# Three attentions of a four-layer transformer kernel: groups that alternate, instead of layer after layer

## The chip, the cores and the metric

The kernel runs on one core of a Trainium2 chip. The metric is device time in microseconds (us), the median of several runs. A core has five engines that each work through their own list of instructions in order: PE (TensorE, matmuls, with a weight load PEld beside it), DVE (VectorE), ACT (ScalarE), POOL (GpSimd) and SP (SyncE, which here only issues DMAs). A line number such as L561 is a line of the kernel before the change.

## The reference, cut to what matters

`x` has 32 sequences of 128 tokens and 128 features. Four layers follow one another, each an attention and a feed-forward, added through a tanh gate. The change touches layers 0 and 1 alone:

```
x = x + tanh(g) * L0_xattn(ctx, layernorm(x), bias, seq_len)   # 16 heads of 8, keys and values from ctx, masked by length
x = x + tanh(g) * L0_ffn(layernorm(x))                        # 128 -> 512 -> 512 -> 512 -> 128, SiLU gate, two GELUs
x = x + tanh(g) * L1_xattn(layernorm(x), ctx, w_qkv, w_proj)  # 16 heads of 8, keys = ctx and own, so 256 keys
x = x + tanh(g) * L1_ffn(layernorm(x))                        # begins with a causal attention, 16 heads of 4, then 2 of 8 experts
...                                                           # layer 2 (attention, experts) and layer 3
```

A sequence depends on no other, up to the experts. So the work on one group of sequences can go ahead of another's, as long as each group passes the steps in order.

## The kernel before, in words

**Groups and jobs.** The 32 sequences are eight groups of four (`NB`). A job is one attention for one group. The loop `attend` (L916) takes a list of jobs. Before, it is 24 jobs, layer by layer: layer 0's attention for groups 0 to 7, then layer 1's for 0 to 7, then the causal one inside layer 1's feed-forward (called 1f) for 0 to 7.

**A job** (`attention`, L536) has four units of four heads and two steps a unit, so eight steps. A step first computes scores (PE `sc` L561; a causal row L584 first in 1f) for the maxima (DVE L592 or L597). The maxima are split in three bfloat16 parts, transposed (`tpn` L611) and written by a DMA into rows 96 to 98 of the query tile (L615), so that a second product of the same parts, with keys and queries exchanged (`sct` L561), gives scores less their maximum. ACT takes the exponential (L627); in 1f POOL then sets the later positions to zero (L630); PE multiplies with the values (`av` L644), whose extra column of ones gives the sum, and the result is divided (L650 to L659). Layer 1's steps have two score tiles instead of one.

**Operand tiles.** Queries and keys are kept in DRAM as three bfloat16 parts and loaded as stacks (`Stacks.load`, L386) into ring buffers (`Slots`, L346): four query tiles `stack_q` and four each of `stack_k` and `stack_l`. Rows 0 to 71 (0 to 35 in 1f) hold the parts. In layer 0, rows 72 to 74 of the key hold the bias and masks; the query rows 64 to 95 hold ones. As the three layers share the tiles, the first jobs of layer 1 and of 1f have POOL set rows to zero (`ready` and `take`, L360 to L370).

**The pipe** (`Pipe`, L446) sets the order. `turn` (L486) runs once a step: weights four steps after the scores, products one step after that, one step of `before` (the preparation of the next job: normalization, projections, splitting in parts), one of `after` (what follows a finished job), and `beside` (L479), which takes pieces of the `fill`. The fill is layer 0's feed-forward (`mlp0`, L1012): it is appended when a group's first attention is done. It yields after every eight rows or so of matmul: SiLU pairs, then eight GELU pieces (PE L1037, ACT L1040), then the last product (L1046). At one piece a step it lags behind the attention and ends in layer 1's stage. A layer 1 job for a group can't begin before that group's feed-forward is done (L1068), and a 1f job not before layer 1's job of that group (L1114).

A scheduler then places the emitted instructions in the engines' lists, so that a piece can move some steps from where it was emitted.

**Shared rooms.** `shared` (L936) gives everything but scores and products two psum banks under one tag, `h`: transpositions, projections, the feed-forward. Tag `scr` has two buffers, `y` three.

**Clears.** Each feed-forward piece also issues one DMA of zeros (`cleared`, L995) into the table from which the experts later read, until 40 are out. SP issues these, in order with all loads.

**What follows.** After the 24 jobs come layer 1's experts, layer 2's attention with its own pipe, layer 2's experts, and layer 3.

Of the kernel before, what the change touches and what calls it, by code (L numbers as in the profile page):

```python
# [12 lines left out]
F32 = mybir.dt.float32  # L13
F32R = mybir.dt.float32r
BF = mybir.dt.bfloat16
# [7 lines left out]
P = 128  # L23
NB = 4
# [2 lines left out]
EPS = 1e-5  # L27

LOTS = dict(r1=(0, 8, 512), r2=(0, 8, 512))
MAGIC = 12582912.0  # L30


# [40 lines left out]
def tile_flamingo_gated(  # L73
# [20 lines left out]
    nc = tc.nc  # L94
    B = x.shape[0]
    NG = B // NB
# [16 lines left out]
    xs = []  # L113
# [23 lines left out]
    ones = CST(cst, "ones")  # L137
# [52 lines left out]
    with tc.tile_pool(name="prep", bufs=1) as pp, tc.tile_pool(name="prep_ps", bufs=2, space=PSUM) as ppp:  # L190
        for name, bias in (("bias0", bias0), ("bias2", bias2)):
            parts = pp.tile([P, 3, B], BF, tag=f"parts_{name}", name=f"parts_{name}")
            rest = pp.tile([P, B], F32, tag="rest", name=f"rest_{name}")
            split3(parts[:, 0], parts[:, 1], parts[:, 2], bias, rest)
            tp = ppp.tile([3 * B, P], BF, tag="tp", name=f"tp_{name}")
            nc.tensor.transpose(tp, parts.rearrange("p a b -> p (a b)"), ident_b)
            rows = pp.tile([3 * B, P], BF, tag=f"rows_{name}", name=f"rows_{name}")
            nc.vector.tensor_copy(rows, tp)
            kept = dram.tile([3, B * P], BF, name=f"kept_{name}")
            nc.sync.dma_start(out=kept.rearrange("a (b k) -> (a b) k", k=P), in_=rows)  # L200
            bias_rows[name] = kept


    def rsqrt(pool, v, eps=EPS):
# [141 lines left out]
    class Slots:  # L346


        def __init__(self, pool, name, n, blocks=4, ones=(96, 99), engines=(nc.vector, nc.gpsimd)):
            self.at, self.tiles, self.readied = 0, [], {}  # L350
            for i in range(n):
                t = pool.tile([P, blocks, NB, P], BF, name=f"stack_{name}{i}", bufs=1)
                eng = engines[i % len(engines)]
                rows = t.rearrange("p m b k -> p (m b k)")
                eng.memset(rows, 0.0)
                if ones:
                    eng.memset(rows[ones[0] : ones[1]], 1.0)
                self.tiles.append(t)

        def ready(self, rows, value):  # L360

            for i in range(len(self.tiles)):
                self.readied.setdefault(i, []).append((rows, value))

        def take(self):
            i = self.at % len(self.tiles)
            self.at += 1
            for rows, value in self.readied.pop(i, []):
                nc.gpsimd.memset(self.tiles[i].rearrange("p m b k -> p (m b k)")[rows], value)
            return self.tiles[i]  # L370

    class Stacks:

# [2 lines left out]

        def __init__(self, H, d, queries, keys, bias=None, readied=()):

            self.bias, self.slots, self.readied = bias, [queries] + keys, readied
            self.H, self.halves = H, max(1, d // 8)
            self.d = d // self.halves
            self.ahead = {}

        def load(self, n, parts, at, group):  # L386

            t = self.slots[n].take()
            heads = slice(0, 9 * self.d)
            for e in range(self.halves):  # L390
                dst = t[heads, 4 * e : 4 * (e + 1)]
                if n == 0:
                    first = (self.H * e + 4 * at) * NB * P
                    src = parts.rearrange("d c h n -> (d c) (h n)")[:, first : first + 4 * NB * P]
                    nc.sync.dma_start(
                        out=dst.rearrange("p m b k -> p (m b k)"),
                        in_=src[:, None, :].to_broadcast([3 * self.d, 3, 4 * NB * P]),
                    )
                else:
                    src = parts.rearrange("(h e) d a (c n) -> e (d a c) h n", e=self.halves, n=NB * P)[e]  # L400
                    nc.sync.dma_start(
                        out=dst.rearrange("p m b k -> p m (b k)"), in_=src[:, 4 * at : 4 * (at + 1)]
                    )
            if n and self.bias:
                rows = bias_rows[self.bias][:, group * NB * P : (group + 1) * NB * P]
                nc.sync.dma_start(
                    out=t[72:75, 0:4].rearrange("p m b k -> p m (b k)"),
                    in_=rows[:, None, :].to_broadcast([3, 4, NB * P]),
                )
            return t  # L410

        def loads(self, group, q, keys, at):
            for slots, rows, value in self.readied:
                slots.ready(rows, value)
            self.readied = ()
            return self.load(0, q, at, group), [self.load(i + 1, k, at, group) for i, k in enumerate(keys)]


# [117 lines left out]
    def attention(banks, r, g, q, keys, values, o, following=None, causal=False):  # L536
# [18 lines left out]
        def product(dst, stat, mov, b, start, whole):  # L555

            n = r.halves
            for h in range(4):
                for e in range(n):
                    rows = slice(0, P if whole and e == n - 1 else 96)  # L560
                    nc.tensor.matmul(  # L561
                        dst[:, h * P : (h + 1) * P], lhsT=stat[rows, 4 * e + h, b], rhs=mov[rows, 4 * e + h, b],
                        start=start and h == e == 0, stop=h == 3 and e == n - 1, skip_group_check=True,
                    )

        def unit(u):
# [41 lines left out]
            def placed(negp, dq):  # L608

                tp = psum.tile([48, P], BF, tag="tp", name="tpn")  # L610
                nc.tensor.transpose(tp, negp.rearrange("p c x -> p (c x)"), ident_b)  # L611
                rows = pool.tile([48, P], BF, tag="mrows", name="mrows")
                nc.vector.tensor_copy(rows, tp)
                first = 4 * (r.halves - 1)
                nc.sync.dma_start(  # L615
                    out=dq[96:99, first : first + 4].rearrange("p h b q -> p (h b) q"), in_=rows
                )

            def weights(bp):
# [283 lines left out]
    class Layer:  # L903

        def __init__(self, stacks, before, given, after, causal=False, ahead=1):

            self.ahead = ahead
            self.stacks, self.before, self.given, self.after, self.causal = stacks, before, given, after, causal  # L910

        def begin(self, g):
# [3 lines left out]
    def attend(pipe, banks, jobs):  # L916
# [8 lines left out]
        for i, (layer, g) in enumerate(jobs):  # L925
            if i in ends:
# [2 lines left out]
            parts = attention(  # L929
                banks, layer.stacks, g, *layer.given(g), (lambda: then.begin(n)) if then else None, layer.causal  # L930
            )
            due = jobs[i + 1 : i + 1 + layer.ahead] if i == 0 else jobs[i + layer.ahead : i + 1 + layer.ahead]
            pipe.run(parts, chain(*[a.before(m) for a, m in due]), lambda layer=layer, g=g: layer.after(g))
        pipe.drain()
# [39 lines left out]
    with ExitStack() as stack:  # L974
# [11 lines left out]
        def layer0():  # L986
# [2 lines left out]
            h1 = W0(w0, "h1").rearrange("p (c o) -> p c o", c=4)  # L989
            h2 = W0(w0, "h2").rearrange("p (c o) -> p c o", c=4)  # L990
            w3 = W0(w0, "w3").rearrange("p (c o) -> p c o", c=4)
            zeros = mlp.tile([P, 512], F32, name="zeros")
            nc.gpsimd.memset(zeros, 0.0)

            def cleared():  # L995
                if clear:
                    t = clear.pop(0).rearrange("n p m -> p n m")
                    nc.sync.dma_start(out=t, in_=zeros[:, None, 0 : t.shape[2]].to_broadcast(list(t.shape)))

            def before(g):  # L1000
                y = layernorm(pool, xs[g], bufs=3)
                kT = pool.tile([P, NB * P], F32, tag="xT", name="kT", bufs=1)
                nc.sync.dma_start(out=kT, in_=ctx_kT[:, g * NB : (g + 1) * NB, :])
                yield
# [5 lines left out]
                at[g] = q, [k], [va], o  # L1010

            def mlp0(g):  # L1012
                y = layernorm(pool, xs[g], bufs=3)
                yield
                xT = mlp.tile([P, NB * P], F32, tag="xT", name="xT")
                nc.vector.tensor_copy(xT, flat(transposed(psum, y)))
# [38 lines left out]
                return  # L1055
                yield

            return Layer(stacks, before, lambda g: at[g], after)

        done = set()  # L1060

        def layer1():
            stacks = Stacks(16, 8, queries, [keys0, keys1], readied=[(queries, slice(64, 96), 0.0)])
            qkv = WA(wa, "qkv")
            at = {}

            def before(g):
                while g not in done:  # L1068
                    pipe.advance(pipe.fill)
                y = layernorm(pool, xs[g], bufs=3)  # L1070
                yield
                xT = pool.tile([P, NB, P], F32, tag="xT", name="xT", bufs=1)
                nc.scalar.copy(xT, transposed(psum, y))
# [29 lines left out]
                add_gated(xs[g], 1, po)  # L1103
                done.add(8 + g)

            return Layer(stacks, before, lambda g: at[g], after)

        def layer1f():
            cleared = [(keys1, slice(i, i + 32), 0.0) for i in (32, 64)]
            stacks = Stacks(16, 4, queries, [keys1], readied=cleared)  # L1110
            at = {}

            def before(g):
                while 8 + g not in done:  # L1114
                    pipe.advance(pipe.afters)
                y, h = layernorm(pool, xs[g], bufs=3, again="scr")
                yield
                hT = pool.tile([P, NB, P], F32, tag="scr", name="hT")
                nc.scalar.mul(hT, transposed(psum, h), COL(col, "g1"))
# [51 lines left out]
                    nc.tensor.matmul(pl[:, b, :], lhsT=tT[:, b, :], rhs=WA(wa, "router"), start=True, stop=True)  # L1171
                yield from routes1.take(pool, psum, g, pl, t, 5, 0.0)

            return Layer(stacks, before, lambda g: at[g][:4], after, causal=True)

        layers = layer0(), layer1(), layer1f()
        attend(pipe, banks, [(layer, g) for layer in layers for g in range(NG)])


    tail = ctx.enter_context(tc.tile_pool(name="tail", bufs=1))  # L1180
# [448 lines left out]
```

## Time and profile before

| what | us |
|---|---|
| median of 3 runs (2176.64 to 2182.37) | 2178.75 |
| the profiled execution, time | 2170.34 |
| its span | 2168.5 |
| PE busy in the span (76%) | 1658.0 |
| DVE busy (55%) | 1197.4 |
| ACT busy (41%) | 894.0 |
| POOL busy (29%) | 638.6 |
| ACT table loads ahead of exponentials, 72 of them | 92.4 |
| 16 DMA engines, share of their time for SP's queue | 34.0% |

A page gives busy time per engine, then the span in 40 slices with a digit for the busy tenths and for the granted clock of PE. The trace answers for a stretch of time, and lists groups of instructions as "line engine operation out<-in, count | busy us, mean ns | idle before, and what ended it". A wait is listed as who waited for whom, with its total us, how often, and the longest. In a busy PE row the ends of matmuls are modelled, so that rows overlap; the distance of two starts tells the pace.

### The profile page before, as it was taken

The numbers are of one execution on the slowest core, as the hardware profiler recorded it, in microseconds if no ns is written. First come the engines' busy times: TensorE is split into PE (matmuls) and PEld (weight loads), VectorE is DVE, ScalarE is ACT, GpSimd is POOL, SyncE is SP. The second block draws the span as 40 slices with busy tenths as digits, with TensorE's granted clock in tenths as the row PEclk, the third lists the DMA queues.
The fourth block names the chain that finished last, engine by engine and source line by source line (L and its number), as shares of the span: only waits on it lengthen the run. The fifth ranks groups of instructions, "written<-read, shape, count | busy, mean of one in ns | idle before, by whom it ended". The sixth has DMA issues, their size and how long they took to land.

```text
span 2168.5 us, 35498 instructions
## 1 busy us (share of the span) xinstructions
PE 1658.0 (76%) x13624; PEld 1010.3 (47%) x13624; DVE 1197.4 (55%) x3504; ACT 894.0 (41%) x1110; POOL 638.6 (29%) x637
## 2 busy tenths in 40 slices
PE   0599998989999999878777569926666629995355
PEld 0455445456656666555455424414555514442223
DVE  7645446475545476766666433357667631113797
ACT  0376565565787745333323223301111204441244
POOL 5101101020000012454544482056443430003550
PEclk9999999999999999987877779966667759997566
DMA  6564558634332343112212035435344212332110
GB/s 214 154 230 154 187 184 266 219 101 124 105 100 67 94 145 84 51 54 59 56 48 55 25 116 174 141 104 148 110 124 121 71 63 101 135 132 86 41 49 20
DMA packets 164536, 244.66 MB, mean 113 GB/s; under 512 B 20560, under 2 KB 102288, under 8 KB 164112
## 3 DMA queue, kind: packets, MB, share of 16 engines
q1 hardware_dynamic: 156176, 225.62, 34.0%
q0 software_dynamic: 8192, 16.79, 2.7%
q8 instruction: 107, 1.75, 0.4%
q14 instruction: 61, 0.50, 0.1%
HBM read 139.74 MB, written 101.24 MB: 111 GB/s over the span
## 4 chain that ended last, share of the span: by engine, by line
PE 40%; DVE 14%; POOL 13%; issue 8%; ACT 2%; DMA 2%; SPq 0%; POOLq 0%; DVEq 0%; ACTq 0%
PE ye L851 5%; PE ph L1382 4%; PE av L644 4%; POOL by_expert_r L699 4%; PE sct L561 4%; POOL got L886 3%; PE sc L561 3%; PE ph L1037 3%; PE p L1203 2%; PE tpe L838 2%; DVE mx L592 2%; PE p L1205 2%; PE tp L282 1%; POOL r L208 1%; POOL w L249 1%
## 5 line engine op out<-in xcount | busy, mean ns | idle before, releaser
L627 ACT ACTIVATE w<-sct 128x1024 f32<-128x1024 f32 x288 | 292.8, 1024 | 346.4 <-PE sct L561 345.2
L592 DVE TENSOR_REDUCE mx<-sc 128x8 f32<-128x1024 f32 x160 | 194.9, 1220 | 130.0 <-PE sc L561 129.6
L561 PEld LDWEIGHTS <-stack_q 96*128 96x128 bf16 x2560 | 194.4, 110 | 134.5 <-issue 104.3
L886 POOL DMA_INDIRECT got<-by_expert_r,slot_r x128 | 127.7, 998 | 360.8 <-issue 335.0
L597 DVE TENSOR_REDUCE mx<-sc 128x4 f32<-128x1024 f32 x128 | 152.9, 1222 | 132.8 <-PE sc L561 132.3
L644 PE MATMUL av<-w,va 128*9 128x128 f32 (+2 forms) x3584 | 198.1, 295 | 36.7 <-POOL w L630 31.9
L561 PE MATMUL sc<-stack_k,stack_q 96*128 96x128 bf16 x1536 | 145.7, 244 | 46.8 <-DMA stack_k<-k 17.4
L561 PE MATMUL sct<-stack_q,stack_k 128*128 128x128 bf16 (+1 forms) x1536 | 139.5, 236 | 17.3 <-DVE mx L592 8.3
L561 PEld LDWEIGHTS <-stack_k 128*128 128x128 bf16 (+1 forms) x1536 | 111.8, 107 | 69.6 <-issue 66.6
L644 PEld LDWEIGHTS av<-w,va 128*9 128x9 f32 (+2 forms) x3584 | 98.6, 94 | 87.5 <-POOL w L630 43.5
L851 PE MATMUL ye<-hid,w 128*128 128x512 f32 x276 | 133.4, 593 | 2.3 <-DVE hid L1208 2.3
L311 POOL CAST hml<-whole 128x512 bf16<-128x512 f32 (+1 forms) x48 | 30.1, 626 | 343.0 <-ACT whole L310 166.7
L1037 PE MATMUL ph<-h,w 128*128 128x512 f32 x256 | 123.7, 610 | 1.8 <-ACT hn L1040 0.9
L1037 PE MATMUL ph<-hn,w 128*128 128x512 f32 x256 | 121.2, 604 | 0.7 <-ACT hn L1040 0.7
L208 POOL TENSOR_TENSOR r<-r,m 128x4 f32<-128x4 f32 x56 | 58.5, 1044 | 188.8 <-DVE r L207 175.0
L561 PE MATMUL sc<-stack_l,stack_q 96*128 96x128 bf16 x1024 | 110.4, 238 | 0.0
L650 ACT COPY ot<-av 128x512 f32<-128x512 f32 x112 | 65.5, 584 | 99.5 <-PE av L644 96.6
L630 POOL TENSOR_SCALAR_AFFINE_SELECT w<-w 128x1024 f32<-128x1024 f32 x64 | 70.8, 1106 | 113.9 <-ACT w L627 113.7
L561 PE MATMUL sct<-stack_q,stack_l 128*128 128x128 bf16 x1024 | 98.9, 234 | 2.7 <-DVE mx L592 2.7
L627 ACT ACT_TABLE_LOAD x72 | 92.4, 1283 | 9.7 <-PE sct L561 8.5
L699 POOL DMA_INDIRECT by_expert_r<-yn,slot_r x64 | 65.6, 1025 | 83.1 <-DVE slot_r L757 25.4
L656 PE MATMUL tpo<-cst,ot 128*128 128x128 f32 x448 | 82.4, 306 | 9.5 <-ACT ot L650 6.9
(295 smaller groups left out, 3290.5 us busy)
## 6 DMA issues: line engine op xcount, KB each, us to landing
by_expert_r<-zeros SPq DMA_DIRECT2D x40, 1024.0 KB
stack_q<-q SPq DMA_DIRECT2D x96, 288.0 KB
stack_k<-k SPq DMA_DIRECT2D x96, 288.0 KB
k<-hml SPq DMA_DIRECT2D x16, 1152.0 KB
w<-in_e_dram SPq DMA_DIRECT2D x23, 514.5 KB
xt<-by_expert_r SPq DMA_DIRECT2D x46, 256.0 KB
by_expert_r<-yt SPq DMA_DIRECT2D x46, 256.0 KB
q<-hml SPq DMA_DIRECT2D x72, 128.0 KB
```

Source lines behind the costliest of these rows:

```text
L208: nc.gpsimd.tensor_tensor(r, r, m05.to_broadcast([P, NB]), ALU.pow)
L561: nc.tensor.matmul(dst[:, h * P : (h + 1) * P], lhsT=stat[rows, 4 * e + h, b], rhs=mov[rows, 4 * e + h, b], start=start and h == e == 0, s ...
L592: latest["maxima"] = nc.vector.tensor_reduce(mx[:, :, b0 : b0 + 2].rearrange("p h b -> p b h"), sc.rearrange("p i (h k) -> p i h k", h=4), ...
L597: nc.vector.tensor_reduce(mx[:, :, b0], sc.rearrange("p i (h k) -> p h i k", h=4), AX.XY, ALU.max, negate=True,)
L627: latest["weights"] = nc.scalar.activation(w.rearrange("p i h k -> p i (h k)"), sc, AF.Exp)
L644: nc.tensor.matmul(av[32 * h : 32 * h + dv + 1, b * P : (b + 1) * P], lhsT=values[c][:, b, 4 * u + h, :], rhs=w[:, i, h, :], start=c == 0, ...
L656: nc.tensor.transpose(tp[:, b].rearrange("p s r -> p (s r)"), ot[:, b, :], ident)
L699: ins = nc.gpsimd.indirect_dma_start(out=self.rows(), out_offset=bass.IndirectOffsetOnAxis(ap=slots, axis=0), in_=rows, in_offset=None,)
L851: nc.tensor.matmul(y, lhsT=w2[:, f, :], rhs=hid[:, f, :], start=f == 0, stop=f == n_f - 1)
L886: ins = nc.gpsimd.indirect_dma_start(out=got[:, k, b, :], out_offset=None, in_=self.rows(), in_offset=bass.IndirectOffsetOnAxis(ap=self.sl ...
L1037: nc.tensor.matmul(ph, lhsT=wt[:, c, f * P : (f + 1) * P], rhs=h[:, c, :], start=c == 0, stop=c == 3)
L1382: nc.tensor.matmul(ph, lhsT=E2(w, "w1")[:, f * P : (f + 1) * P], rhs=xT, start=True, stop=True)
```

## The change

1. **Order.** The 24 jobs are no longer layer by layer but in the list `ORDER`: five of layer 0, then jobs of layer 1, layer 0 and 1f in turn; it ends with three of 1f.
2. **Rates.** `beside` takes 0.875 pieces a step in jobs of layer 0 and of 1f and 0.5 in jobs of layer 1, instead of 1.
3. **Shared tiles.** As the layers now use the tiles in turn, POOL zeroes no rows between the stages any more: every load of layer 1's first key tile also brings three rows of zeros, and every load of 1f's key brings three rows of ones at rows 36 to 38, where 1f's maxima now go. Its products take 36 and 39 rows instead of 96 and 128. POOL's twelve memsets are gone; two small DRAM rows of zeros and ones are made at the start.
4. **Clears.** The tile of zeros has 256 columns instead of 512, and each clear is two DMAs of half the size.
5. **Buffers.** `y` has four buffers instead of three.

```
+ORDER = [
+    (0, 0), (0, 1), (0, 2), (0, 3), (0, 4), (1, 0), (0, 5), (1, 1), (2, 0), (1, 2), (0, 6), (1, 3),
+    (2, 1), (1, 4), (0, 7), (2, 2), (1, 5), (2, 3), (1, 6), (2, 4), (1, 7), (2, 5), (2, 6), (2, 7),
+]
+RATES = 0.875, 0.5, 0.875
...
+        for name, value in (("zeros", 0.0), ("ones", 1.0)):
+            rows = pp.tile([3, NB * P], BF, tag=f"rows_{name}", name=f"rows_{name}")
+            nc.vector.memset(rows, value)
+            bias_rows[name] = dram.tile([3, NB * P], BF, name=f"kept_{name}")
+            nc.sync.dma_start(out=bias_rows[name], in_=rows)
...
-            for rows, value in self.readied.pop(i, []):
-                nc.gpsimd.memset(self.tiles[i].rearrange("p m b k -> p (m b k)")[rows], value)
...
+            self.parts = 9 * self.d
+            self.top, self.end, self.all = (36, 36, 39) if self.d == 4 else (96, 96, P)
...
-            if n and self.bias:
-                rows = bias_rows[self.bias][:, group * NB * P : (group + 1) * NB * P]
+            if n and self.beside[n - 1]:
+                rows = bias_rows[self.beside[n - 1]]
+                if rows.shape[1] > NB * P:
+                    rows = rows[:, group * NB * P : (group + 1) * NB * P]
                 nc.sync.dma_start(
-                    out=t[72:75, 0:4].rearrange("p m b k -> p m (b k)"),
+                    out=t[self.parts : self.parts + 3, 0:4].rearrange("p m b k -> p m (b k)"),
...
-                    rows = slice(0, P if whole and e == n - 1 else 96)
+                    rows = slice(0, r.all if whole and e == n - 1 else r.end)
...
+            pipe.fills[0] = (pipe.fill, layer.rate)
...
-            zeros = mlp.tile([P, 512], F32, name="zeros")
+            zeros = mlp.tile([P, 256], F32, name="zeros")
...
-                    t = clear.pop(0).rearrange("n p m -> p n m")
-                    nc.sync.dma_start(out=t, in_=zeros[:, None, 0 : t.shape[2]].to_broadcast(list(t.shape)))
+                    t = clear.pop(0).rearrange("n p (i m) -> i p n m", m=256)
+                    for half in (t[0], t[1]):
+                        nc.sync.dma_start(out=half, in_=zeros[:, None, :].to_broadcast(list(half.shape)))
...
-                y = layernorm(pool, xs[g], bufs=3)
+                y = layernorm(pool, xs[g], bufs=4)
...
-            return Layer(stacks, before, lambda g: at[g], after)
+            return Layer(stacks, before, lambda g: at[g], after, rate=RATES[0])
...
-            stacks = Stacks(16, 8, queries, [keys0, keys1], readied=[(queries, slice(64, 96), 0.0)])
+            stacks = Stacks(16, 8, queries, [keys0, keys1], "zeros", None)
...
-            cleared = [(keys1, slice(i, i + 32), 0.0) for i in (32, 64)]
-            stacks = Stacks(16, 4, queries, [keys1], readied=cleared)
+            stacks = Stacks(16, 4, queries, [keys1], "ones")
...
-        attend(pipe, banks, [(layer, g) for layer in layers for g in range(NG)])
+        attend(pipe, banks, [(layers[i], g) for i, g in ORDER])
```

## The prediction

> **What bounds it now.** I read the page's 40 slices first, then busy time by stage, then the stretches job by job, then PE's waits. Jobs are one attention for one group; I cut the stages at the first exponential (ACT w L627) of each layer: layer 0's attention 71.3 to 480.4, layer 1's to 881.8, layer 1's second ("1f", causal) to 1225.7, everything later 942.8 us.
>
> ```profile
> PE   0599998989999999878777569926666629995355
> PEclk9999999999999999987877779966667759997566
> ```
>
> Slices 2 to 16 are full of PE at the whole clock; slices 17 to 23 (1f) are not. Busy time by stage (columns: stretch, its us, busy us of PE, PEld, DVE, ACT, POOL, granted clock, DMA share, GB/s):
>
> ```profile
> 71.30:480.40 409.10, 369.14 (x2827) 202.83 (x2826) 219.14 (x585) 248.32 (x270) 49.78 (x68) 0.97 0.57 187
> 480.40:881.80 401.40, 385.37 (x4690) 253.70 (x4687) 240.01 (x510) 266.76 (x295) 52.07 (x68) 1.00 0.37 101
> 881.80:1225.70 343.90, 270.21 (x2599) 176.26 (x2595) 221.70 (x718) 110.37 (x150) 168.23 (x168) 0.81 0.19 51
> 1225.70:2168.50 942.80, 622.33 (x3452) 369.67 (x3452) 467.52 (x1590) 263.98 (x391) 335.34 (x298) 0.76 0.33 100
> ```
>
> No other engine is over 70% in any of the first three. PE is the bound in layers 0 and 1; in 1f PE is short of ready work and runs at 0.81. Why, from PE's waits in 1f (total, times, longest):
>
> ```profile
> PE av L644 <- POOL w L630: 30.5, 27, 3.4
> PE sc L584 <- DVE mx L592: 12.7, 14, 3.8
> PE tp L282 <- DVE t L1165: 9.7, 7, 2.7
> ```
>
> These are chains (exponential, POOL's causal mask, product) with nothing independent between. The feed-forward of layer 0 is independent, but it is used up by 757 us.
>
> **PE work at full clock.** Recorded durations overlap, so I count by the distance of starts, in layer 1's timeline:
>
> ```profile
> 607.67 3.65 PE L1037 MATMUL ph<-h,w 128*128 128x512 f32 x8
> 611.15 0.33 PE L561 MATMUL sc<-stack_k,stack_q 96*128 96x128 bf16 x3
> ...
> 616.87 0.39 PE L561 MATMUL sc<-stack_k,stack_q 96*128 96x128 bf16 x4
> 617.09 0.39 PE L561 MATMUL sc<-stack_l,stack_q 96*128 96x128 bf16 x4
> ```
>
> 3.48 us for eight fp32 rows of 512: 0.43 each (3.44 a piece of eight). 0.22 for four score rows: 0.056 each. Likewise av 0.037, fp32 rows of 128 0.11, tpn 0.17, the causal row of 512 0.22. One feed-forward group has 88 rows of 512 and 8 transposes: 37.8+0.9 = 38.7 us, in 11 pieces. A job of layer 0: 128 score rows 7.2, 128 av 4.7, 20 transposes 2.2, tpn 0.7 = 14.8. Layer 1: 256 scores 14.3, 256 av 9.5, transposes 2.6, projections 3.5, tpn 0.7 = 30.6. 1f: 7.2+4.7, 16 masks 3.5, transposes 3.1, projections 4.3+2.6, tpn 0.7 = 26.1. Layer 1's stage holds 184 of the 512 rows of L1037, so 2.9 of eight feed-forwards; layer 0's 5.1. Filling of PE by stage: (118+197)/409 = 77%; (245+112)/401 = 89%; 209/344 = 61%.
>
> What a job costs without any feed-forward: layer 0 33.5 (the first one), layer 1 (39.4+42.2+39.1)/3 = 40.2, 1f a mean of 45.7 over seven, and 23.9 for the last. The covered stretch 104.8 to 757.2 (layer 0's jobs 1 to 7, layer 1's 0 to 4, all feed-forwards) holds 104+153+310 = 567 us of work in 652.4 us: 87%.
>
> **The change, part by part.** *The order and the rates.* Nothing of the attention or feed-forward work is added or removed; pieces move. In the order in which the changed program issues ACT's instructions I counted SiLU pairs and GELUs between the exponentials: of 80 such pieces 45 stand in layer 0's jobs, 18 in layer 1's, 17 in four 1f jobs ((2,0) to (2,3): 4, 6, 4, 3). The last piece is in (2,3). So 18 jobs are covered; six are not: (1,6), (2,4), (1,7), (2,5), (2,6), (2,7). Before, eight 1f jobs and about three of layer 1 were bare. Sum: job (0,0) 33.5; the other 17 covered jobs hold 7x14.8+6x30.6+4x26.1+310 = 702 us. At 85% filling that is 826. Bare: 2x40.2+3x45.7+23.9 = 241. Together 1100.5 against 1154.4: -54. I take 85%, under the 87% shown, because a covered 1f job brings its POOL chain; at 93% (layer 1's stretch 519.8 to 757.2: 122+112 in 237, near 99%, shows that high is possible) it is 755: -125; at 78% (layer 0's stage) 900: +20.
>
> *The covered 1f job closely:* 26.1+17/4x3.44 = 41 us of work against 45.7 bare, if the clock comes back to that of covered jobs (0.97 to 1.00). If it stayed 0.81, the four jobs' 162 us of work would be 200: +38. I take the former, since layer 1's stage ran at 1.00.
>
> *ACT.* The two programs have 150 table loads each, so the sum does not change, but GELUs now stand among 1f's exponentials, which POOL's masks and then PE wait for:
>
> ```profile
> L1040 ACT ACT_TABLE_LOAD x30 | 38.5, 1283 | 0.5
> L1040 ACT ACTIVATE hn<-ph,col 128x512 f32<-128x512 f32 x41 | 28.2, 687 | 45.4 <-PE ph L1037 45.2
> ```
>
> A piece costs ACT up to 0.69+2x1.28 = 3.3 us, 14 in a 1f job that has 14.5: 28 of 48. The Trainium skill, page "ScalarE: Activation LUTs", section "Table sets: the hidden batching unit", speaks against the change: activations should be batched by table set, and it gives about 2.7 us a load. By its figure a piece is 6.1, the job 14.5+26 = 40 of 48, and ACT would nearly bind (my 85% would fall to about 80%). The trace's 1.28 decides.
>
> *POOL.* 1f's 64 scatters (L699, 1.07 us each, 8.5 a job) stand among its masks; a 1f job's scatters fall due in the job after it, which for (2,0) to (2,4) is one of layer 0 or 1 without masks. A gain of up to 8 us over these jobs that I leave inside the 85%.
>
> *Clears.* 40 transfers of 1 MB become 80 of 0.5 MB with packets of 1 KB instead of 2 KB. The trace's packets in this stretch took 91 ns (2 KB) and 60 ns (1 KB): 20,480x91/16 = 116 us of the 16 engines' time becomes 154, +38 over some 400 us whose share is 0.57. Hidden behind PE while the share stays under 1; where it is a burst, stack_k and stack_q loads queue behind it. Bounds 0 and +15; I take +2. SP: 40 more issues at 0.50 and 64 row loads (zeros or ones for the keys) at 0.33: 41 us on a queue that spends 341 of 1154 issuing. A row load follows the key load of a tile that is wanted two units later; behind it on SP stand the maxima (stack_q<-mrows) and the next unit's loads, which PE's sct wants four steps later, so I take 0 (up to +6: 64 landings, each 0.1 late). Three clears now stand ahead of the first q and k writes behind the weights' load: 0 to +5, I take +2.
>
> *Stacks.* Twelve POOL memsets of 1.8 us go (4 at 433 to 475, 8 at 848 to 881); they held SP's stack_q loads up to 18 us, but PE's rows show no wait on them: 0 (down to -6). Score rows in 1f contract 36 or 39 partitions instead of 96 or 128; rows of 96 and 128 both took 0.22 us, so 0. y gets a fourth buffer, which keeps 1f's held residual from blocking: 0. Two DVE memsets at the start, under 0.5 each: +1.
>
> Sum: -54+5 = -49. Against the profiled execution (span 2168.5, time 2170.3) that is 2121; the median of the runs is 8.4 above the profiled one, so 2130.
>
> **Rivals.**
> *A, main case (0.58):* filling 82 to 89%, 2093 to 2163.
> *B, more (0.12):* mixed jobs fill as layer 1's stretch did, 93% and over: 2059 to 2093. For it: 97 to 99% has been reached. Against: layer 0's jobs with as many pieces had 84%.
> *C, the pieces pay in 1f what they paid before (0.14).* In layer 0 57 pieces cost 409-8x33.5 = 141: 2.5 each, 72% of their PE time although a bare job left PE idle for half. If they cost 2.5 in 1f and the clock gives nothing back, the sum is only the +5 of side costs: 2184; with half of the clock back (6 us a job, four jobs, halved: -12) 2172. Of its 0.14, 0.06 lies under 2172, 0.07 within 0.3%, 0.01 above.
> *D, slower (0.16): psum.* Two banks, tag h, serve every transposition, projection and feed-forward product of all three layers. A covered 1f job takes them some 12 times for itself and 5 or 6 for pieces, where a bare one took 12, and a bank is held until ACT or DVE, in order behind exponentials, has read it. PE is in order: a wait for a bank holds the scores behind it. At 0.7 us more for each of 4x18 uses the -50 is gone; at 1.0, 72-49 = +23: 2202. Against: layer 1's covered jobs took them some 15 times in 59 us with almost no PE wait.
> *That the order isn't followed:* excluded by the issue order above: the jobs alternate and the pieces are spread.
>
> **Numbers.** A measurement tells 0.3%, 6.5 us. Faster: A, B and 0.06 of C = 0.76. Within: 0.07 of C and 0.02 of D = 0.09. Slower: 0.01 of C and 0.14 of D = 0.15. The range leaves out half of B (0.06) and most of D above 2190 (0.12): 2080 to 2190.
>
> **What would show it.** Right: the attention stages end at about 1177 instead of 1225.7; slices with 1f jobs (2,0) to (2,3) show PE at 9 and a clock over 0.93; the last three 1f jobs look as before, 45 us each at about 0.8; table loads unchanged. Wrong: covered 1f jobs over 55 us; PE rows that wait on ACT hn or ACT sil (D); clock near 0.8 in mixed slices; DMA share near 1 and PE waiting on stack_k or stack_q in the first 400 us; the late stages, unchanged in code, longer than 943 us.

## The result, and the profile after

The change makes the kernel slower. Median of four runs 2272.77 us (2270.17 to 2277.51), against 2177.69 for the kernel before on the same chip: ratio 1.0434, 95% interval 1.0413 to 1.0455. The profiled execution took 2277.5, its span is 2275.5. The forecast was 2130, at the other side of no change. The median of the kernel before was between 2167.6 and 2170.7 on some occasions (e1 to e12 and e18 below) and between 2177.7 and 2179.4 on others (this run, e13 to e17). So in what follows a run's us over the kernel before are its ratio times 2178. The expectations were written in the shorter times; against them the medians of e13 to e17 are to be read as some 10 us lower.

The same two rows of 40 slices of the changed kernel, with the granted clock in the second:

```profile
PE   0698888887999899898899939954666646997444
PEclk9899999987999899999765559985766667998566
```

Counted from 0, slices 2 to 18 show PE at 7 to 9 tenths, nearly all at a clock of 9 tenths or more. Slices 19 to 22 are new: PE at 8 and 9, at a clock of 5 to 7 tenths. That is not an engine short of work, which is how I had read 1f before; it is an engine at about half speed.

By stage (stretch, its us, busy us of PE, PEld, DVE, ACT, POOL, clock, DMA share, GB/s): job (0,0), the seventeen covered jobs (with pieces of the feed-forward beside them), the six bare ones (without), all later work.

```profile
72.10:110.90 38.80, 27.50 (x287) 18.36 (x286) 24.66 (x77) 14.34 (x17) 4.47 (x6) 0.84 0.41 122
110.90:1014.80 903.90, 820.48 (x7489) 480.42 (x7487) 494.91 (x1253) 518.35 (x577) 153.84 (x195) 0.95 0.43 127
1014.80:1316.00 301.20, 267.55 (x2322) 159.43 (x2320) 159.66 (x484) 94.81 (x120) 88.98 (x91) 0.66 0.19 51
1316.00:2275.50 959.50, 628.02 (x3462) 373.53 (x3468) 467.89 (x1589) 263.97 (x392) 334.34 (x297) 0.76 0.32 99
```

Forecast for the first three: 33.5, 826 and 241. Measured: +5, +78, +60; later work +17. The last three 1f jobs, which I had expected "as before, 45 us each at about 0.8", one a row:

```profile
1168.40:1232.60 64.20, 61.34 (x408) 31.77 (x400) 27.21 (x69) 15.94 (x22) 17.18 (x18) 0.53 0.18 43
1232.60:1284.80 52.20, 44.76 (x319) 25.75 (x319) 24.19 (x79) 12.06 (x16) 17.60 (x17) 0.50 0.12 35
1284.80:1316.00 31.20, 28.73 (x218) 17.30 (x217) 15.51 (x62) 10.54 (x13) 10.27 (x10) 0.50 0.01 4
```

PE is at work in 61.34 of 64.20 us, at 0.53. Its waits in the bare stretch (total, times, longest) name nothing that could be worth 60 us, and no psum bank:

```profile
PE tpo L662 <- ACT ot L656: 6.0, 9, 0.8
PE sct L567 <- DVE mx L603: 4.8, 3, 3.4
PE tp L294 <- DVE t L1172: 3.8, 3, 2.2
PE tpn L617 <- DVE negp L174: 3.6, 2, 3.4
```

What became slow shows in the distance of starts. The kernel before, in its first 1f job at the full clock: causal row, four score rows, and again (start, us, engine, line, operation):

```profile
915.75 0.39 PE L584 MATMUL sc<-cbf 128*128 128x512 bf16 x1
915.98 0.39 PE L561 MATMUL sc<-stack_l,stack_q 96*128 96x128 bf16 x4
916.20 0.38 PE L584 MATMUL sc<-cbf 128*128 128x512 bf16 x1
916.42 0.39 PE L561 MATMUL sc<-stack_l,stack_q 96*128 96x128 bf16 x4
```

The changed kernel, in the third 1f job from the end, (2,5):

```profile
1173.70 0.61 PE L590 MATMUL sc<-cbf 128*128 128x512 bf16 x1
1174.24 0.61 PE L567 MATMUL sc<-stack_l,stack_q 36*128 36x128 bf16 x4
1174.78 0.61 PE L590 MATMUL sc<-cbf 128*128 128x512 bf16 x1
1175.32 0.61 PE L567 MATMUL sc<-stack_l,stack_q 36*128 36x128 bf16 x4
```

0.45 us for a causal row and its four products has become 1.08. Half the clock explains a factor of two (0.90); the rest is new.

### The profile page after: what moved, and what is told of

Same layout as the page of the kernel before. It is cut to its first block, busy times and chain, and to the rows that moved or that the text cites. A ratio compares the mean times of both kernels' runs of the same rounds, so it can differ in the third digit from the quotient of the medians.

```text
span 2275.5 us, 35555 instructions
## 1 busy us (share of the span) xinstructions
PE 1754.6 (77%) x13618; PEld 1039.6 (46%) x13624; DVE 1197.9 (53%) x3506; ACT 896.0 (39%) x1110; POOL 615.4 (27%) x625
## 4 chain that ended last, share of the span: by engine, by line
PE 56%; DVE 16%; issue 10%; POOL 10%; ACT 3%; DMA 3%; SPq 1%; another core or an unknown queue 1%; POOLq 0%; DVEq 0%; ACTq 0%
PE ph L1045 8%; PE av L650 7%; PE sc L567 6%; PE sct L567 6%; PE ye L857 5%; PE ph L1389 4%; POOL got L892 3%; PE tpo L662 2%; POOL by_expert_r L705 2%; DVE mx L603 2%; PE p L1210 2%; PE sc L590 2%; PE tpe L844 2%; DVE mx L598 2%; POOL r L220 2%
## 5 line engine op out<-in xcount | busy, mean ns | idle before, releaser
L567 PEld LDWEIGHTS <-stack_q 96*128 96x128 bf16 (+1 forms) x2560 | 188.8, 111 | 158.8 <-issue 130.0
L650 PE MATMUL av<-w,va 128*9 128x128 f32 (+2 forms) x3584 | 209.5, 306 | 23.2 <-POOL w L636 10.1
L567 PE MATMUL sc<-stack_k,stack_q 96*128 96x128 bf16 x1536 | 151.2, 249 | 53.7 <-DMA stack_k<-k 16.0
L567 PE MATMUL sct<-stack_q,stack_k 128*128 128x128 bf16 (+1 forms) x1536 | 148.4, 242 | 35.6 <-DVE mx L603 12.6
L567 PEld LDWEIGHTS <-stack_k 128*128 128x128 bf16 (+1 forms) x1536 | 117.2, 110 | 86.2 <-issue 81.8
L650 PEld LDWEIGHTS av<-w,va 128*9 128x9 f32 (+2 forms) x3584 | 103.3, 96 | 72.9 <-issue 26.7
L567 PE MATMUL sc<-stack_l,stack_q 36*128 36x128 bf16 (+1 forms) x1024 | 113.4, 242 | 0.0
L567 PE MATMUL sct<-stack_q,stack_l 39*128 39x128 bf16 (+1 forms) x1024 | 107.5, 246 | 7.5 <-DVE mx L603 6.2
L662 PE MATMUL tpo<-cst,ot 128*128 128x128 f32 x448 | 89.7, 327 | 19.2 <-ACT ot L656 17.2
L633 ACT ACT_TABLE_LOAD x73 | 93.7, 1283 | 10.4 <-PE sct L567 5.4
L567 PEld LDWEIGHTS <-stack_l 39*128 39x128 bf16 (+1 forms) x1024 | 77.1, 110 | 29.8 <-issue 24.6
```

Source lines behind the costliest of these rows:

```text
L567: nc.tensor.matmul(dst[:, h * P : (h + 1) * P], lhsT=stat[rows, 4 * e + h, b], rhs=mov[rows, 4 * e + h, b], start=start and h == e == 0, s ...
L633: latest["weights"] = nc.scalar.activation(w.rearrange("p i h k -> p i (h k)"), sc, AF.Exp)
L650: nc.tensor.matmul(av[32 * h : 32 * h + dv + 1, b * P : (b + 1) * P], lhsT=values[c][:, b, 4 * u + h, :], rhs=w[:, i, h, :], start=c == 0, ...
L662: nc.tensor.transpose(tp[:, b].rearrange("p s r -> p (s r)"), ot[:, b, :], ident)
```

## The experiments

My theory after this look (N in the expectations): the narrow products of 1f (36 and 39 rows), which I had costed at nothing, are the loss, and the order's gain is small. Rivals: the order itself is slower (O); the lower piece rates starve PE; the clears, the row loads or the fourth `y` hold something up.

| run | what | median | ratio, 95% interval |
|---|---|---|---|
| e1_wide | change, wide products | 2202.0 | 1.0151 (1.0134 to 1.0168) |
| e2_layerwise | change, old order and rates | 2282.1 | 1.0528 (1.0511 to 1.0546) |
| e3_layerwise_wide | both | 2209.4 | 1.0193 (1.0176 to 1.0210) |
| e4_rate1 | change, old rates | 2241.8 | 1.0356 (1.0321 to 1.0392) |
| e5_before_narrow | before, narrow products with their ones loads | 2267.8 | 1.0465 (1.0447 to 1.0482) |
| e6_before_clears_y4 | before, half clears, fourth `y` | 2165.2 | 0.9989 (0.9980 to 0.9999) |
| e7_layerwise_wide_y3 | e3, three `y` | 2202.1 | 1.0153 (1.0135 to 1.0171) |
| e8_wide_rate1 | e1, old rates | 2200.6 | 1.0150 (1.0120 to 1.0180) |
| e9_scores36 | before, 1f's scores alone at 36 rows | 2196.8 | 1.0134 (1.0098 to 1.0171) |
| e10_scores64 | the same at 64 rows | 2199.3 | 1.0156 (1.0111 to 1.0201) |
| e11_noff_alternating | e1 without the feed-forward | 2088.6 | 0.9640 (0.9604 to 0.9676) |
| e12_noff_layerwise | e3 without the feed-forward | 2094.5 | 0.9661 (0.9629 to 0.9694) |
| e13_sct96 | e5, weights' product at 96 rows | 2251.9 | 1.0340 (1.0305 to 1.0374) |
| e14_sct64 | e5, at 64 rows | 2269.0 | 1.0410 (1.0377 to 1.0443) |
| e15_masks_first | e5, causal rows of both halves first | 2256.0 | 1.0347 (1.0329 to 1.0364) |
| e16_before_rows1 | before, layer 1's rows of zeros loaded | 2182.4 | 1.0013 (1.0002 to 1.0024) |
| e17_before_wide_rows | before, 39 rows of zeros loaded in 1f | 2209.7 | 1.0133 (1.0112 to 1.0154) |
| e18_sct128 | e5, at 128 rows | 2234.0 | 1.0283 (1.0245 to 1.0322) |

**Products wide again, in both orders** (e1, e3), and the old order with narrow ones (e2). As 1f shares its key tiles, wide products need rows of zeros under the keys, which these kernels load with each tile (36 rows instead of 3 of ones):

```
-            self.top, self.end, self.all = (36, 36, 39) if self.d == 4 else (96, 96, P)
+            self.top, self.end, self.all = 96, 96, P
...
-            stacks = Stacks(16, 4, queries, [keys1], "ones")
+            stacks = Stacks(16, 4, queries, [keys1], "wide")
```

The old order is `ORDER = [(i, g) for i in range(3) for g in range(8)]` with `RATES = 1, 1, 1`.

> The changed kernel, with 1f's products back at 96 and 128 partitions: instead of three rows of ones, each of 1f's key loads brings 36 rows of zeros, and its maxima go to rows 96 to 98 again. Theory N (the narrow products of 36 and 39 rows cost the most: a product after one of another height starts about 0.09 us later, 40 times a job, some 30 us in all; and in the bare last jobs they hold PE at half clock, 60 us there): the attentions end near 1226 to 1240 instead of 1316, the last three jobs take about 45, 45 and 24 us at 0.7 to 0.9 of the clock instead of 64, 52 and 31 at 0.5, and the whole is 2180 to 2200. Theory O (the order costs it: mixed jobs fill PE badly, whatever the height): within 15 us of 2273.

> The changed kernel with the old order, layer by layer, and one piece a step; all else of the change stays: narrow products in 1f, rows of zeros and ones, halved clears, four y buffers. Theory N: eight bare 1f jobs with narrow products at half clock, so worse or as bad: 2250 to 2330, 1f's stage about 420 to 480 us instead of 344 at a clock of 0.5 to 0.6. Theory O: the old order gives the old time, 2175 to 2195.

> Old order, one piece a step, and 1f's products at 96 and 128 partitions by 36 rows of zeros a load: what remains of the change are the row loads, the halved clears, the fourth y and the missing memsets. Both theories: 2175 to 2190, near the kernel before. If it is over 2200, clears and row loads cost something that neither has.

Widening gives back 62 us in the new order (1.0434 to 1.0151) and 73 in the old (1.0528 to 1.0193). The new order with its rates is worth 20 us where the products are narrow (1.0528 to 1.0434) and 9 where they are wide (1.0193 to 1.0151). So the order isn't the loss, and its gain is far under the 54 of the forecast. e3 missed its 2175 to 2190 by 20 us; e6, e7, e16 and e17 look for what is left in it.

In the profile of e1 the covered jobs take 880.2 us instead of 903.9, and the six bare ones, at a higher clock, 257.2 instead of 301.2:

```profile
990.80:1248.00 257.20, 208.66 (x2322) 138.99 (x2321) 164.01 (x485) 93.71 (x120) 87.23 (x90) 0.83 0.26 68
```

**The rates alone** (e4, e8): `RATES = 1, 1, 1` in the change and in e1.

> The changed kernel with one piece of the feed-forward a step everywhere, so that it is used up sooner. Theory N: more 1f jobs are bare with narrow products: 2285 to 2310. Theory O, in the form that the alternation itself is bad and the rate of no weight: 2260 to 2285.

> The alternating order with wide products and one piece a step. With narrow products one piece a step was 31 us faster than 0.875 and 0.5. If fewer pieces a step cost in themselves, 2165 to 2180, which would be the first to reach the kernel before. If that gain came of fewer pieces beside narrow products, 2195 to 2215.

With wide products nothing (1.0150 against 1.0151); with narrow ones the old rates are 17 us faster (1.0356 against 1.0434), where both theories had it no faster than 2260. Fewer pieces a step never helped; why they cost beside narrow products was not looked into.

**The narrow products alone, in the kernel before** (e5): the three edits of 1f and no other.

```
+            self.top, self.end, self.all = (36, 36, 39) if self.d == 4 else (96, 96, P)
...
-                    rows = slice(0, P if whole and e == n - 1 else 96)
+                    rows = slice(0, r.all if whole and e == n - 1 else r.end)
...
-            stacks = Stacks(16, 4, queries, [keys1], readied=cleared)
+            stacks = Stacks(16, 4, queries, [keys1], "ones")
```

> The kernel before with one edit alone: 1f's products take 36 and 39 partitions (three rows of ones come with each of its key loads, its maxima go to rows 36 to 38, no memsets for 1f). Theory N (the narrow products are the cause, by themselves): 1f's stage 410 to 440 us instead of 344 at a clock near half, the whole 2235 to 2265. If narrow products only hurt together with the other edits: within 10 us of 2169.

+101 us, just over what N had said: more than the whole loss. Layers 0 and 1 take what they took. 1f, from 880 to 1330 us and with what drains after it, in the same columns as above:

```profile
880.00:1330.00 450.00, 390.00 (x2641) 209.03 (x2635) 228.48 (x718) 112.12 (x151) 174.40 (x174) 0.57 0.15 42
```

0.57, where the old 1f had 0.81. Its jobs take 50 to 62 us instead of 42 to 49, the last one left out.

**The side edits** (e6: half clears and a fourth `y` in the kernel before; e7: e3 with three `y`).

> The kernel before with the two edits that go with each other's room: 80 clears of half the size with packets of 1 KB, and a fourth y buffer. The layerwise kernel with wide products is some 40 us above the kernel before, and its layer 0 stage is as long as that of before, so clears should cost nothing: 2165 to 2180. If the fourth y lets the scheduler move work so that 1f's stage gets worse, 2190 to 2205.

> The layerwise kernel with wide products and three y buffers again; row loads and halved clears stay. If the fourth y is what costs the 40 us: 2165 to 2180. If it is the row loads in place of memsets (or the order of issue that they bring): 2200 to 2215 as with four.

e6 is 2 us faster than the kernel before. In the layer by layer kernel the fourth `y` costs 9 (1.0193 against 1.0153), in the kernel before it doesn't; I did not find why.

**Which product, and by its rows or by its neighbours** (e9, e10, then e13, e14, e18, e15). Two theories: a product costs more next to one of another height ("neighbours", later H), or the clock falls with the rows that the products leave idle ("gate", later C). L is that the loads of the ones rows cost. e9 and e10 narrow the scores' product in 1f and load nothing:

```
+            self.end = 36 if self.d == 4 else 96
...
-                    rows = slice(0, P if whole and e == n - 1 else 96)
+                    rows = slice(0, P if whole and e == n - 1 else 96 if whole else r.end)
```

> The kernel before with one edit: in 1f the scores for the maxima (sc) take 36 partitions, the other product (sct) stays at 128. No load and no memset changes. Theory gate (rows of the array that a product leaves idle count as idleness for what sets PE's clock): the clock in 1f falls well under 0.81, to some 0.65 to 0.7, 1f's stage is 370 to 410 us, the whole 2195 to 2230. Theory neighbours (only the 0.09 us after a change of height costs): the clock stays about 0.8, 32 changes a job are 3 us, partly hidden, the whole 2168 to 2190.

> As the run with scores of 36 partitions, but 64. Theory gate: between the kernel before and the run with 36, the clock 0.7 to 0.8, 2175 to 2205. Theory neighbours: the same start-to-start cost as with 36 if any height under 96 has it, and then the same time as with 36; or the time before.

36 and 64 rows cost the same within their intervals, 29 and 34 us. e9's time and clock (0.69 over 1f and 0.62 over its middle, against 0.81 and 0.77 in the kernel before) are those that the gate theory had. That 64 rows are no faster, at a little higher clock (0.68 over the middle), speaks for the neighbours. The causal row and four products in e9, same place and clock as shown of the kernel before:

```profile
915.79 0.39 PE L585 MATMUL sc<-cbf 128*128 128x512 bf16 x1
916.11 0.39 PE L562 MATMUL sc<-stack_l,stack_q 36*128 36x128 bf16 x4
916.43 0.39 PE L585 MATMUL sc<-cbf 128*128 128x512 bf16 x1
916.76 0.39 PE L562 MATMUL sc<-stack_l,stack_q 36*128 36x128 bf16 x4
```

Recorded lengths are the old ones (0.39), so the groups of the page show nothing; the starts are 0.32 apart instead of 0.22. Each change between 128 rows and 36 costs 0.1 us. Four products beside one another still follow at 0.056. 1f has 128 such pairs: 128x0.19 = 24 us at the full clock, more at half. That is near the measured 29, but the clock fell too, and e9 does not part the two.

e13, e14 and e18 are e5 with more rows in the weights' product (`self.all` 96, 64 and 128; the added rows hold zeros in the keys). e15 issues both halves' causal rows ahead of both halves' products, so that two of four changes go:

```
-                    for i, (b, c) in enumerate(halves):
-                        if causal:
+                    for i in range(2 if causal else 0):
...
+                    for i, (b, c) in enumerate(halves):
                         product(sc[:, i], dq, ks[c], b, not causal, False)
```

> The kernel before with layer 1f's score products at 36 rows, its ones rows loaded and its query rows moved as the change has them, but the product for the weights at 96 rows in place of 39 (rows 39 to 96 of the keys hold zeros). Theory H (a product of 64 rows or fewer beside one of 128 costs a step, and 96 rows do not) and theory C (the granted clock falls with the rows that the products use): as with the scores alone narrowed, 2190 to 2205. Theory L (what both narrow products cost beyond the scores alone, some 70 us, is the loading of the ones rows ahead of each key tile): 2255 to 2270.

> As the run with 96 rows, but 64 rows in the product for the weights. H: 64 and 39 are on the same side of the step, so as with 39: 2260 to 2275. C, if the clock goes with the number of rows: between, 2225 to 2245. L: 2260 to 2270.

> The kernel before with both of layer 1f's products narrow (36 and 39 rows), and the causal masks of both halves of a score tile issued ahead of both halves' products: mask, mask, products, products in place of mask, products, mask, products. Two of four changes of height in each of 64 tiles go. H: 128 changes at 0.10 us at the full clock and up to twice that at half: 12 to 25 us less than with the old order, 2243 to 2256. C: the same products at the same heights, 2263 to 2270.

> As the run with 96 rows in the product for the weights, but all 128 (the rows from 39 on hold zeros in the keys), so that against the kernel before only the scores' 36 rows, the ones rows loaded ahead of each key tile and the place of the maxima are left. Reading of the run with 96 rows: the loads cost some 45 us there and 96 rows stand beside 128 for nothing: ratio 1.031 to 1.037 again. If it is instead 96 beside 128 that costs in this product: near the run with the scores alone at 36 rows, ratio 1.011 to 1.018.

e15 gives back 26 us (1.0465 to 1.0347), a little over the 12 to 25 of H; the rows in use are the same and the clock hardly moves (0.57 to 0.59), so the steps between neighbours cost by themselves and C alone is out. e14 came nearer to H than to C. e13 missed the figure of both by some 40 us and lies nearer to L's. e18 fell between its own two cases. The larger part of e13's miss is the loading of the ones rows (with the maxima's place, which moves with it): e18 is +32 over e9. By the ratios the weights' product then costs +12, +15 and +12 as it goes from 128 to 96, 64 and 39 rows. Only 96 to 64 crosses the step, and by the length of 1f itself, from its first exponential to its last, most of the cost lies there (kernel before 343.9, then e9, e18, e13, e14, e5 and e15):

```profile
881.90:1251.30 369.40, 325.61 (x2591) 190.11 (x2587) 218.50 (x714) 110.65 (x150) 168.58 (x169) 0.69 0.17 47
886.10:1285.40 399.30, 335.62 (x2573) 190.74 (x2573) 230.93 (x714) 109.91 (x148) 168.38 (x168) 0.67 0.16 45
885.20:1293.80 408.60, 344.94 (x2573) 194.75 (x2573) 231.20 (x713) 110.06 (x148) 167.57 (x165) 0.64 0.16 44
881.90:1311.60 429.70, 370.63 (x2574) 200.83 (x2572) 228.87 (x713) 110.09 (x148) 166.86 (x166) 0.59 0.15 42
881.20:1316.80 435.60, 383.55 (x2577) 204.94 (x2576) 227.05 (x713) 110.29 (x148) 166.46 (x166) 0.57 0.15 42
879.10:1299.10 420.00, 354.16 (x2577) 198.97 (x2575) 229.57 (x713) 110.41 (x148) 167.09 (x166) 0.59 0.16 43
```

That is +26 for the scores, +30 for the ones rows, then +9, +21 and +6, and 16 back in e15; one profile each. By the distance of starts at half clock the step is clean: weights' product to causal row 0.107 (128 rows), 0.106 (96), 0.243 (64), 0.243 (39). What else moves is the clock over the middle of 1f: 0.66 (e18), 0.62 (e13), 0.57 (e14, e5). How much of the cost is the steps and how much the clock stays open.

**The row loads alone** (e16: layer 1's three rows of zeros; e17: the zeros under 1f's keys that e1, e3, e7, e8, e11 and e12 load, here 39 rows, in place of the one clearing).

```
-            stacks = Stacks(16, 4, queries, [keys1], readied=cleared)
+            stacks = Stacks(16, 4, queries, [keys1], "wide")
```

> The kernel before, only that layer 1's three zero rows are loaded ahead of each key tile, as in the change, where they were cleared once. If such loads cost nothing, as predicted: 2165 to 2173. If they are part of what layer by layer order with all of the change has above the kernel with narrow products alone (14 us): 2176 to 2185.

> The kernel before, only that layer 1f's 39 zero rows are loaded ahead of each key tile, as (with 36 rows) in my runs with wide products, where before cleared them once. If the 33 us by which those runs stay above the kernel before are these loads, which the change itself does not have: 2195 to 2205. If they lie in the change's own edits: 2167 to 2175.

Layer 1's loads cost 3 us by the ratio, as good as forecast (2182.4 stands against 2179.1 for the kernel before). e17's cost 29, so most of the 33 us by which e1 stays above the kernel before can be put down to loads that I had added to make it; e17 has the old order, so for the new one this is not shown. As the narrow products bring a load that costs as much (32), the 62 and 73 us that widening gave back would be the products' own; they lie near 29+39 = 68, what the scores (e9) and the weights' product (e18 to e5) cost apart.

In e17 1f is 23 us longer than in the kernel before, with much the same PE work. Bandwidth is not short (DMA share 0.25). One chain of delay (start, us, engine, line):

```profile
1018.04 3.02 DVE L167 TENSOR_TENSOR negp<-mrest,negp 128x16 bf16<-128x16 f32 x1
1018.71 1.28 POOL L1144 TENSOR_TENSOR rt<-rt 64x512 f32<-64x512 f32 x1
1019.92 1.10 POOL L636 TENSOR_SCALAR_AFFINE_SELECT w<-w 128x1024 f32<-128x1024 f32 x1
1021.11 0.24 PE L617 MATMUL tpn<-cbf,negp 128*48 128x128 bf16 x1 [2.58 <-DVE negp L167]
```

The last step of the maxima's splitting, 0.16 us in the kernel before, lasts until POOL's two operations end, and PE's transposition waits for it. Over 1f the 90 operations that write `negp` take 36 us instead of 19. In e13 they take 23, so that this does not explain the ones loads' 32; how these lengthen 1f stays open.

**Without the feed-forward** (e11, e12): e1 and e3, where layer 0's feed-forward is left out; its pieces issue their clears only.

```
             def mlp0(g):
                 yield
+                for i in range(10):
+                    cleared()
+                    yield
                 done.add(g)
```

> The alternating order with wide products, with layer 0's feed-forward left out (its clears and its place in the order stay; the output lacks it). Against 2202 with it. The prediction's term: mixed jobs hide pieces better, so that leaving them out saves less than in the old order: 2202 less 150 = 2050. The rival C of the prediction (pieces cost 2.5 us each wherever they stand, 88 of them): 2202 less 220 = 1980, and the same bare time as in the old order.

> The old order with wide products and the feed-forward left out, against 2209 with it. From the profile before, 57 pieces in layer 0 cost 141 us and 31 in layer 1 cost 77: 2209 less 218 = 1991. If the alternating order is faster with feed-forward for its cover alone, it is no faster here; if alternation costs by itself, this one is the faster of the two without feed-forward, by 30 us or more.

Both came some 40 to 110 us above their expectations. The eight feed-forwards, 310 us of PE work, save 2202.0-2088.6 = 113 us when left out of the new order and 2209.4-2094.5 = 115 in the old one, 1.3 us for each of 88 pieces. These are lower bounds, for something else then holds the jobs up. e12 by stage, layer 0's jobs 1 to 7, layer 1's, 1f's, and PE's waits for loads in the first of the three (total, times, longest):

```profile
105.70:403.20 297.50, 189.43 (x2028) 135.21 (x2026) 153.60 (x369) 84.76 (x104) 30.13 (x48) 0.65 0.76 241
403.20:770.40 367.20, 313.75 (x4442) 221.53 (x4441) 239.64 (x463) 165.63 (x198) 37.44 (x60) 0.93 0.42 112
770.40:1138.20 367.80, 280.82 (x2566) 179.25 (x2565) 243.43 (x711) 108.14 (x147) 166.34 (x166) 0.79 0.23 60
```

```profile
PE sc L565 <- DMA stack_k<-kept_bias: 33.1, 7, 12.5
PE sc L565 <- DMA stack_k<-k: 12.0, 2, 9.7
PE sct L565 <- DMA stack_q<-mrows: 4.0, 1, 4.0
```

PE stands for its operands, most likely as the clears come closer together there (DMA share 0.76): 54 us over all jobs of e12 and 19 of e11, where e1 has 1 and e3 none. So the pieces cost at most 113+19 = 132 us in the new order and 115+54 = 169 in the old one (estimates, if every wait were pure loss). Whether the new order hid more of them and lost that elsewhere isn't settled; the whole gives it 9 to 20 us.

A layer 0 job without pieces takes 297.5/7 = 42.5 us in e12, or 35.5 without these waits (an estimate), a layer 1 job 45.9 with some clears still beside it.

## Why the prediction was wrong, point by point

**"Score rows in 1f contract 36 or 39 partitions instead of 96 or 128; rows of 96 and 128 both took 0.22 us, so 0."** The step that failed worst. 0 was read from rows on one side of a step and used on the other. Measured: +29 for the scores (e9), +39 for the weights' product from 128 to 39 rows (e18 to e5): some 68 us. In the changed kernel most of it lies in the bare jobs, which I had at their old length (301.2 against 241; 257.2 with wide products). The trace of before shows no product of 36 rows beside one of 128, and I put no bound on either side of that 0.

**"A row load follows the key load of a tile that is wanted two units later ... so I take 0 (up to +6)."** Right for layer 1 (3). Wrong for the ones rows of 1f: +32 (e18 over e9, with the maxima's place), though they are 12 KB.

**"702 us. At 85% filling that is 826", the order's -54.** 702 us took 903.9 (78%), and with wide products 880.2 (80%, e1): the low case of the prediction (78%: 900, +20) and not the one taken. Whole to whole the order with its rates gave -20 (after against e2) or -9 (e1 against e3). The mis-sized term is the filling: 85% was taken from a stretch whose layer 1 part ran near 99%, and the mixed jobs filled as layer 0's stage had. What keeps them there the runs do not show. Rival C, that a piece pays in 1f what it paid before, has e11 and e12 for it as they stand (1.3 us either way, half its price of 2.5), but with the waits for loads taken off they allow 1.5 against 1.9.

**The clock of the covered 1f jobs** came back as taken: (2,1), (2,2) and (2,3) ran at 1.00, 0.97 and 0.98 in 47.4, 53.1 and 46.6 us; only (2,0) at 0.75 in 71.5. It is the bare jobs, which I had not looked at twice, that fell to 0.66.

**Clears +2, fourth `y` 0:** together -2 in e6. **ACT's tables:** 73 loads ahead of exponentials, 93.7 us, against 72; right. **Rival D (psum):** the sign came true, the mechanism did not: over the covered jobs PE waited 0.4 us for `hn` and `sil` together. **The late stages "unchanged":** +17. Layer 2's attention, from its first exponential to its last, took 268 us instead of 259, with code that nobody touched. It took 267 to 270 in e13 to e17 too, beside which the kernel before itself took 2179, and 257 to 261 in e1, e2, e5, e9 and e18, beside which it took 2168 to 2171; the profile of before is one of 2170. So these 9 us go with the occasion and not with the change. The rest is open.

The sum as measured: +101 (e5) +14 (all other edits at old order, e2 over e5, of which 3 are layer 1's loads and the rest isn't apportioned) -20 (order and rates) = +95. It meets the whole by construction, since each run is compared with the next; along another path the shares differ. None of the runs with all the work in it beats the kernel before by a margin that counts. The order with wide products and no added loads would be near the kernel before (an estimate: 33 of e1 less 29 of e17 is +4); it wasn't tried.

## What to carry to other kernels

An operand made "smaller" is not free: give a product of other height than its neighbours a price from both sides, and read it from the distance of starts, as recorded lengths don't move. What a piece of filler costs is better measured by leaving it out than from the one job that happens to be bare; but then look whether what is left is held up by something else, as here by loads that came late. Take the filling of a mixed stretch from the part that it resembles, not from an average with a better one. A control that needs an addition of its own (here rows of zeros) has to be run with the addition alone before its remainder is read.

## What the hardware showed that was not expected

- A product on 64 rows or fewer next to one on 96 or more costs about 0.1 us at each change (0.056 to 0.148 and 0.22 to 0.32 at the full clock, 0.107 to 0.243 at half); 36 next to 39 (0.106 to 0.107 at half clock in e5), 39 next to 64 (0.107, e15) or 96 next to 128 (0.055 at the full clock, before) cost nothing. It does not show before products with few columns of weights: from a score row to `tpn` (48 columns) it is 0.146 after 36 rows and 0.148 after 96, from the weights' product to `av` (5 columns) 0.240 to 0.245 at half clock after 39, 64, 96 or 128.
- The granted clock stood at 0.50 to 0.57 through stretches in which PE was busy 86 to 96% of the time. The Trainium skill (TensorE: Matmul & The Clock Gate, "Part 1: The HAM clock gate") lets the clock follow how busy PE has been; read with PE's busy row alone, these stretches should have had the full clock. Whether the steps or the rows in use pull it down, the runs do not settle.
- A DVE operation of 0.16 us with two inputs lasted 3.02 beside two POOL operations. It agrees with the Trainium skill (SBUF — State Buffer, "Who interferes with whom"): such an operation and a POOL operation that reads SBUF exclude one another.
- A load of three rows, 12 KB, with each key tile (and the maxima moved to rows 36 to 38) lengthened 1f by some 30 us with a DMA share under 0.2 (e18 against e9); 39 rows alone did it too (29, e17).
